# Sixteen columns in place of one for an accumulator output that nobody reads

## The chip, the cores and the metric

The kernel runs on one core of a Trainium2 chip. The metric is the device time of one execution in microseconds, the median over several runs; smaller is better. The core has five engines with queues of their own: TensorE (PE in the profile; its weight loads are shown apart as PEld), VectorE (DVE), ScalarE (ACT), GpSimd (POOL) and SyncE (SP, which only issues transfers here). Each runs its queue in order, and they wait for one another by semaphores.

## The reference, cut to what matters

The input is `x`, 8 batches of 64 x 16 tokens with 128 channels (1024 tokens per batch). Layer 0 is an attention with 8 heads and two softmaxes in a row, a layer norm, a feed-forward part and a layer norm. Layer 1 is an additive attention over all pairs of tokens, and then a recurrent part over the tokens:

```python
def _L1_attn_ref(B, W, v):
    Wi = jnp.einsum('bnd,ed->bne', B, W)
    scores = jnp.einsum('d,bijd->bij', v, jnp.tanh(Wi[:, None, :, :] + Wi[:, :, None, :]))
    attn = jax.nn.softmax(scores, axis=-1)
    return jnp.einsum('bij,bjd->bid', attn, B)
...
x = _L0_conv_ref(x, ...)
t = _to_tokens(x)
t = t + _L1_attn_ref(_ln_t(t), L1_attn_W, L1_attn_v)
t = t + _L1_ffn_ref(_ln_t(t), L1_ffn_W, L1_ffn_V, L1_ffn_gamma, L1_ffn_beta)
```

The scores of layer 1 need a tanh for every pair of tokens and every channel. They are symmetric in the two tokens, so the kernel computes about half of them: 8 batches x some 524,000 pairs x 128 channels.

## The kernel before

Channels lie on the 128 partitions. For one batch, `wiT` holds the projected tokens, 128 x 1024. A row of layer 1 is one token i: its column of `wiT` is added to the columns of all tokens from i on, the tanh of the sum is taken, and TensorE multiplies by `v` (L1175) and collects the scores of 32 tokens per quarter in the PSUM tile `sa`. The function `group` records the rows in groups of 4 k: k rows for each of four row residues c, where k grows from 1 to 8 as the rows get shorter. All rows of a group lie side by side in a stretch of the SBUF ring `th`, which has room for 20 x 1024 columns.

The sum and the tanh of a row can be made in three ways:

- ScalarE does both in one instruction, the tanh with the token's column as bias (`tanh_row`, L1097).
- GpSimd adds k rows at once with one tensor_tensor (`add_rows`, L1107). ScalarE then takes the tanh of whole filled stretches at once (`wide_tanh`, L1155).
- VectorE adds, for k of 4 or more, k rows with the same tensor_tensor (L1107 again), and for smaller k row by row with tensor_scalar (`add_row`, L1101). L1155 then takes the tanh.

The row-wise form has an `accum_out`: besides the sum, the instruction also writes the total of the row to one column per partition. Nobody reads it. On the chip such an operation is shown as two records, `TENSOR_SCALAR_CACHE_REDUCE` for the row and `DVE_READ_ACCUMULATOR` for the total. The column was the last one of an otherwise little used statistics tile:

```python
unused = stats[5][:, 3, 8:9]
...
nc.vector.tensor_scalar(
    rows(c)[:, r, :], wiT[:, i0 + begin[c] :], w_i(c, r), 0.0, ALU.add, ALU.add, accum_out=unused
)
```

The framework that turns the program into instructions puts a semaphore wait wherever an instruction writes what an earlier one wrote or reads, also where both are on the same engine. An instruction that needs more waits than it can carry gets a separate semaphore instruction (`EVENT_SEMAPHORE`) ahead of it.

Who does which part, and in which order, is settled at build time. The class `Plan` collects all operations of both layers with a cost per engine, a priority and their dependencies; `emit` then plays them through and issues each in the order in which it starts in the plan. So layer 0 of the next batch runs between the groups of layer 1 of this batch. Layer 0's VectorE work is the column sums and divisions of the softmaxes (L946, L947, L950, L963, L964), copies out of PSUM (L865), bias adds (L909), and sums into `zs` (L995); its ScalarE work is the exponentials (L942, L960); GpSimd divides again (L974); TensorE makes the scores (L939), the transposes (L853) and the attention products (L988). In layer 1 ScalarE also takes the exponentials of the finished scores (L1271), VectorE takes the reciprocal of the denominator (L1308), and layer norms run over VectorE (L812, L813, L822) and GpSimd (L816, L817, L827). Transfers hardly matter: the queues' share of the 16 transfer engines is 2.3% of the span.

Batch 0's layer 0 runs alone at the start (to about 400 us); the last batch's layer 1 has no layer 0 beside it (from about 4850 us on); the recurrent part of all batches follows from 5300 us.

Of the kernel before, what the change touches and what calls it, by code (L numbers as in the profile page):

```python
# [11 lines left out]
ALU = mybir.AluOpType  # L12
# [3 lines left out]
P = 128  # L16
# [597 lines left out]
@with_exitstack  # L614
def kernel(ctx: ExitStack, tc: tile.TileContext, a: dict):

    fits = ctx.enter_context(tc.tile_pool(name="flag", bufs=1)).tile(
        [1, 1], mybir.dt.int32, tag="fits", name="fits"
    )
    fast_path(tc, a, fits)
    fit = tc.nc.values_load(
        fits[0:1, 0:1], min_val=0, max_val=1, skip_runtime_bounds_check_because="it is a comparison's result"
    )
    with tc.If(fit == 0):
        names = "x wq wk wv wo bq bk bv bo ln1_g ln1_b w1 b1 w2 b2 ln2_g ln2_b wa va wf vf gamma beta out"
        general_path(tc, *[a[n] for n in names.split()])  # L630
# [3 lines left out]
def fast_path(ctx: ExitStack, tc: tile.TileContext, a: dict, fits):  # L634
# [22 lines left out]
    work = main.enter_context(tc.tile_pool(name="work", bufs=1))  # L657
    psum = main.enter_context(tc.tile_pool(name="psum", bufs=1, space=PSUM))

    def tile_of(pool, name, shape):  # L660
        return pool.tile(shape, F32, tag=name, name=name)

    def ring(name, n, shape, pool=work):
        return [tile_of(pool, f"{name}{i}", shape) for i in range(n)]
# [135 lines left out]
    stats = ring("stat", 7, [P, 4, 9])  # L800
# [36 lines left out]
    count = {"aT": 0}  # L837
# [232 lines left out]

                add(("POOL", 2.2), affine2, r=[kg], w=[kg], pri=L0)

    unused = stats[5][:, 3, 8:9]

    def group(it, at0, r0, k, wiT, all_wi, L1, ROWS, fillers, chain, left, both, first_half):

# [4 lines left out]
        i0 = it * P  # L1081
# [3 lines left out]
        begin = [0 if r0 == 0 else 4 * r0 + c for c in range(4)]  # L1085
# [3 lines left out]
        def rows(c):  # L1089
            return slot()[:, at[c] : at[c + 1]].rearrange("p (r n) -> p r n", r=k)  # L1090

        def w_i(c, r=None):
            j = i0 + 4 * r0 + c
            return wiT[:, j : j + 4 * k - 3 : 4] if r is None else wiT[:, j + 4 * r : j + 4 * r + 1]

        def tanh_row(c, r):
            nc.scalar.activation(rows(c)[:, r, :], wiT[:, i0 + begin[c] :], AF.Tanh, bias=w_i(c, r))  # L1097

        def add_row(c, r):

            nc.vector.tensor_scalar(  # L1101
                rows(c)[:, r, :], wiT[:, i0 + begin[c] :], w_i(c, r), 0.0, ALU.add, ALU.add, accum_out=unused
            )

        def add_rows(eng, c):
            shape = [P, k, w - begin[c]]
            eng.tensor_tensor(  # L1107
                rows(c), wiT[:, i0 + begin[c] :].unsqueeze(1).to_broadcast(shape),
                w_i(c).unsqueeze(2).to_broadcast(shape), ALU.add,
            )  # L1110
# [3 lines left out]
        work = {  # L1114
            "ACT": lambda c: (k * (0.18 + 0.833e-3 * (w - begin[c])), lambda: [tanh_row(c, r) for r in rows_of]),
            "POOL": lambda c: (0.27 + 1.62e-3 * k * (w - begin[c]), lambda: add_rows(nc.gpsimd, c)),
            "DVE": lambda c: (k * (0.21 + 1.05e-3 * (w - begin[c])), lambda: [add_row(c, r) for r in rows_of])
            if k < 4
            else (0.15 + 1.04e-3 * k * (w - begin[c]), lambda: add_rows(nc.vector, c)),
        }  # L1120
# [32 lines left out]
        def wide_tanh(_):  # L1153
# [5 lines left out]
            wide_tanh, r=[("rows", g, c) for c in range(4)], w=[("tanh", g)], pri=ROWS - 0.02,  # L1159
# [418 lines left out]
```

## Time and profile before

| What | Value |
|---|---|
| median of 3 runs | 5390.36 us (5388.69 to 5394.67) |
| profiled execution | 5390.73 us |
| its span | 5388.9 us |
| granted TensorE clock, mean | 0.985 |
| busy share PE, DVE, ACT, POOL | 94%, 92%, 95%, 84% |
| instructions on VectorE | 8448 |
| rows at L1101 | 1822, each with an accumulator read |
| separate semaphore instructions at L1101 | 913 |

The profile is of one execution. A group line names the source line, the engine, the operation and its tiles, then how often it occurs, its busy time and mean duration, and the engine's idle time ahead of it with what ended most of that. The chain of waits is followed back from the last instruction: at each step to what released it, or to the instruction ahead of it on its engine. "issue" in it is time in which the engine waited for nothing that the profile shows.

### The profile page before, as it was taken

The numbers are of one execution on the slowest core, as the hardware profiler recorded it, in microseconds if no ns is written. First come the engines' busy times: TensorE is split into PE (matmuls) and PEld (weight loads), VectorE is DVE, ScalarE is ACT, GpSimd is POOL, SyncE is SP. The second block draws the span as 40 slices with busy tenths as digits, with TensorE's granted clock in tenths as the row PEclk, the third lists the DMA queues.
The fourth block names the chain that finished last, engine by engine and source line by source line (L and its number), as shares of the span: only waits on it lengthen the run. The fifth ranks groups of instructions, "written<-read, shape, count | busy, mean of one in ns | idle before, by whom it ended". The sixth has DMA issues, their size and how long they took to land.

```text
span 5388.9 us, 99191 instructions
## 1 busy us (share of the span) xinstructions
PE 5048.0 (94%) x39173; PEld 2782.9 (52%) x39173; DVE 4961.5 (92%) x8448; ACT 5093.6 (95%) x4180; POOL 4536.0 (84%) x3114
## 2 busy tenths in 40 slices
PE   9999999999999999999999999999999999986567
PEld 6655555555555555555555555555555455542125
DVE  7998999999999999999999999999999999988886
ACT  5489999999999999999999999999999999999994
POOL 2364889988998899989999999989999998986992
PEclk9999999999999999999999999999999999998998
DMA  2000000000000000000000000000000000000001
GB/s 62 1 5 1 1 1 5 1 9 1 1 5 5 5 1 1 5 9 1 1 5 5 5 1 1 5 5 5 1 1 5 5 1 1 5 26 7 1 1 68
DMA packets 27339, 37.71 MB, mean 7 GB/s; under 512 B 2512, under 2 KB 19280, under 8 KB 26864
## 3 DMA queue, kind: packets, MB, share of 16 engines
q1 hardware_dynamic: 24832, 27.99, 1.6%
q8 instruction: 310, 5.08, 0.4%
q10 hardware_dynamic: 1872, 3.16, 0.2%
q14 instruction: 165, 1.35, 0.1%
q0 software_dynamic: 160, 0.13, 0.0%
HBM read 19.22 MB, written 12.06 MB: 6 GB/s over the span
## 4 chain that ended last, share of the span: by engine, by line
PE 67%; DVE 15%; ACT 12%; issue 4%; POOL 1%; DMA 0%; DVEq 0%; SPq 0%; ACTq 0%; POOLq 0%
PE sa L1175 24%; PE m L988 13%; PE sc L939 13%; PE m L853 8%; ACT th L1155 6%; DVE th L1101 6%; ACT th L1097 3%; DVE stat_e L963 2%; PE m L917 2%; PE m L1304 2%; DVE stat_e L946 2%; DVE wx L950 1%; PE m L903 1%; DVE aT L865 1%; PE m L1035 1%
## 5 line engine op out<-in xcount | busy, mean ns | idle before, releaser
L1107 POOL TENSOR_TENSOR th<-wiT 128x536 f32<-128x536 f32 (+58 forms) x2304 | 3342.3, 1486 | 244.6 <-PE sa L1175 222.8
L1155 ACT ACTIVATE th<-th 128x2740 f32<-128x2740 f32 (+54 forms) x971 | 2661.2, 2771 | 23.2 <-DVE th L1107 12.3
L1175 PE MATMUL sa<-th,vpat 128*32 128x512 f32 (+32 forms) x24576 | 2030.6, 462 | 212.5 <-ACT th L1155 187.2
L1101 DVE TENSOR_SCALAR_CACHE_REDUCE th<-wiT 128x512 f32<-128x512 f32 (+60 forms) x1822 | 1587.4, 871 | 140.1 <-PE sa L1175 21.9
L1097 ACT ACTIVATE th<-wiT 128x440 f32<-128x440 f32 (+58 forms) x2056 | 1462.7, 782 | 15.1 <-PE sa L1175 14.9
L1175 PEld LDWEIGHTS sa<-th,vpat 128*32 128x32 f32 x24576 | 662.1, 110 | 1341.8 <-issue 850.5
L974 POOL TENSOR_TENSOR wx<-wx,stat_e 128x1024 f32<-128x1024 f32 x512 | 983.2, 1942 | 403.5 <-DVE stat_e L964 360.4
L939 PE MATMUL sc<-xT,wx 128*128 128x512 f32 x2048 | 982.9, 605 | 15.7 <-DVE wx L950 15.3
L988 PE MATMUL m<-aT,wx 128*128 128x256 f32 x3584 | 829.4, 384 | 11.9 <-DVE aT L865 11.9
L988 PEld LDWEIGHTS m<-aT,wx 128*128 128x128 f32 x3584 | 671.1, 191 | 191.9 <-issue 40.7
L946 DVE TENSOR_REDUCE stat_e<-sc 128x16 f32<-128x1024 f32 x512 | 620.4, 1212 | 28.7 <-ACT sc L942 27.8
L950 DVE TENSOR_TENSOR wx<-sc,stat_e 128x1024 f32<-128x1024 f32 x512 | 623.9, 1219 | 23.3
L865 DVE COPY aT<-m 128x512 f32<-128x512 f32 x927 | 600.4, 674 | 34.5 <-PE m L853 32.1
L853 PEld LDWEIGHTS m<-ident,wx 128*128 128x128 f32 x3940 | 445.8, 141 | 326.0 <-issue 162.8
L963 DVE TENSOR_REDUCE stat_e<-wx 128x128 f32<-128x2048 f32 x256 | 583.3, 2278 | 19.0 <-ACT wx L960 18.1
L853 PE MATMUL m<-ident,wx 128*128 128x128 f32 x3940 | 564.4, 278 | 22.5 <-DVE aT L865 12.9
L942 ACT ACTIVATE sc<-sc 128x1024 f32<-128x1024 f32 x512 | 513.7, 1008 | 75.9 <-PE sc L939 71.0
L939 PEld LDWEIGHTS sc<-xT,wx 128*128 128x128 f32 x2048 | 354.9, 190 | 384.3 <-issue 331.4
L960 ACT ACTIVATE wx<-wx 128x2048 f32<-128x2048 f32 x256 | 487.2, 1903 | 21.6 <-DVE wx L950 21.3
L964 DVE RECIPROCAL stat_e<-stat_e 128x128 f32<-128x128 f32 x256 | 244.0, 953 | 8.8
L917 PEld LDWEIGHTS m<-Wvo,xT 128*128 128x128 f32 x1080 | 135.5, 193 | 47.5 <-issue 20.1
L917 PE MATMUL m<-Wvo,xT 128*128 128x128 f32 x1080 | 147.3, 282 | 6.4 <-DVE aT L865 3.0
(183 smaller groups left out, 2899.0 us busy)
## 6 DMA issues: line engine op xcount, KB each, us to landing
xT<-in_xt_dram SPq DMA_DIRECT2D x8, 512.0 KB, 3.5
th<-in_x_dram SPq DMA_DIRECT2D x8, 512.0 KB, 6.9
parked<-X SPq DMA_DIRECT2D x16, 256.0 KB, 2.3
xr<-parked SPq DMA_DIRECT2D x8, 512.0 KB, 7.7
parked_wx<-bT SPq DMA_DIRECT2D x14, 256.0 KB, 2.0
wx<-parked_wx SPq DMA_DIRECT2D x7, 512.0 KB, 3.2
out_dram<-ot ACTq DMA_DIRECT2D x8, 256.0 KB, 2.2
out_dram<-ot SPq DMA_DIRECT2D x8, 256.0 KB, 2.7
```

The lines of the kernel that those rows point to most:

```text
L853: nc.tensor.transpose(bank[:, i * P : (i + 1) * P], s, ident)
L939: nc.tensor.matmul(sc[:, cols], u[:, qt * P : (qt + 1) * P], xT[:, cols], start=True, stop=True)
L946: nc.vector.tensor_reduce(r1, sc.rearrange("p (m g) -> p g m", g=G), AX.X, ALU.add)
L950: nc.vector.tensor_tensor(e3, sc3, r1.unsqueeze(1).to_broadcast([P, M, G]), ALU.mult)
L963: nc.vector.tensor_reduce(r2, e2.rearrange("p q (m g) -> p q m g", g=G), AX.X, ALU.add)
L974: nc.gpsimd.tensor_tensor(e3, e3, r2[:, q, :].unsqueeze(2).to_broadcast([P, M, G]), ALU.mult)
L988: nc.tensor.matmul(bank()[:, :256], vp[:, t, :], aT[:, t, :], start=t == 0, stop=t == NT - 1)
L1097: nc.scalar.activation(rows(c)[:, r, :], wiT[:, i0 + begin[c] :], AF.Tanh, bias=w_i(c, r))
L1101: nc.vector.tensor_scalar(rows(c)[:, r, :], wiT[:, i0 + begin[c] :], w_i(c, r), 0.0, ALU.add, ALU.add, accum_out=unused)
L1107: eng.tensor_tensor(rows(c), wiT[:, i0 + begin[c] :].unsqueeze(1).to_broadcast(shape), w_i(c).unsqueeze(2).to_broadcast(shape), ALU.add,)
L1155: nc.scalar.activation(slot()[:, a:z], slot()[:, a:z], AF.Tanh)
L1175: nc.tensor.matmul(sa[32 * c : 32 * c + 32, s:s1], vpat[:, 31 - r0 - r : 63 - r0 - r], rows(c)[:, r, s - at0 - begin[c] : s1 - at0 - begin ...
```

## The change

The single column is replaced by a tile of 16 columns, `unused`, and each row that VectorE adds takes the next of them in turn. Nothing else is changed; lines below the edit move by 4, so that L1101, L1107, L1155 and L1175 become L1105, L1111, L1159 and L1179. The new tile has 64 bytes per partition and is allocated ahead of the tiles `stat_e`.

```diff
-    unused = stats[5][:, 3, 8:9]
+    unused = tile_of(work, "unused", [P, 16])
+
+    def next_unused():
+        count["unused"] = (count.get("unused", -1) + 1) % 16
+        return unused[:, count["unused"] : count["unused"] + 1]
...
             nc.vector.tensor_scalar(
-                rows(c)[:, r, :], wiT[:, i0 + begin[c] :], w_i(c, r), 0.0, ALU.add, ALU.add, accum_out=unused
+                rows(c)[:, r, :], wiT[:, i0 + begin[c] :], w_i(c, r), 0.0, ALU.add, ALU.add, accum_out=next_unused()
             )
```

## The prediction

> **What bounds the kernel now.** I read the page's engine shares first, then its costliest groups.
>
> ```profile
> PE 5048.0 (94%) x39173; PEld 2782.9 (52%) x39173; DVE 4961.5 (92%) x8448; ACT 5093.6 (95%) x4180; POOL 4536.0 (84%) x3114
> ...
> PE 67%; DVE 15%; ACT 12%; issue 4%; POOL 1%; DMA 0%; DVEq 0%; SPq 0%; ACTq 0%; POOLq 0%
> ...
> L1101 DVE TENSOR_SCALAR_CACHE_REDUCE th<-wiT 128x512 f32<-128x512 f32 (+60 forms) x1822 | 1587.4, 871 | 140.1 <-PE sa L1175 21.9 <-DVE th L1101 16.1 <-issue 2.9
> ```
>
> PE, ACT and VectorE are all nearly full, so the share alone decides nothing. The row touched by the change, L1101, runs 1822 times; VectorE stands idle 140.1 us ahead of it, and the named releasers explain only 41. The busy time by stretch (PE, PEld, DVE, ACT, POOL, then clock, DMA) says more:
>
> ```profile
> 2500.00:3500.00 1000.00, 986.34 (x7928) 542.19 (x7930) 948.49 (x1612) 994.50 (x741) 945.33 (x666) 1.00 0.01 3
> ...
> 5000.00:5100.00 100.00, 59.71 (x544) 16.20 (x536) 89.04 (x158) 100.00 (x34) 93.04 (x59) 0.98 0.00 1
> ```
>
> ACT is the fullest: 994.5 of 1000 us in mid-kernel, all of 5000 to 5200. From 400 to 5300 us ACT is idle for 85 us in all (4900 less the sum of its stretches); before 400 there are few L1101 rows, after 5300 none. The work given to ACT doesn't change, so the change can win what ACT waits, no more. What ends ACT's waits there:
>
> ```profile
> ACT sc L942 <- PE sc L939: 22.9, 30, 2.8
> ACT th L1097 <- PE sa L1175: 14.5, 8, 5.9
> ACT th L1155 <- DVE th L1107: 12.3, 4, 6.8
> ACT E L1271 <- PE sa L1175: 10.5, 9, 2.1
> ACT th L1155 <- DVE th L1101: 7.6, 15, 1.4
> ACT wx L960 <- DVE wx L950: 5.1, 8, 1.5
> ```
>
> VectorE ends 25.0 us of it directly (12.3 + 7.6 + 5.1), PE 47.9 us.
>
> **How rows follow each other.** The timeline of VectorE (start, duration):
>
> ```profile
> 2614.21 1.01 DVE L1101 TENSOR_SCALAR_CACHE_REDUCE th<-wiT 128x768 f32<-128x768 f32 x1 [0.86 <-PE sa L1175]
> 2615.15 0.08 DVE L1101 DVE_READ_ACCUMULATOR th<-wiT 128x1 f32 x1
> 2615.15 0.69 DVE L865 COPY aT<-m 128x512 f32<-128x512 f32 x1
> ...
> 2635.70 0.08 DVE L1101 DVE_READ_ACCUMULATOR th<-wiT 128x1 f32 x1
> 2635.82 1.00 DVE L1101 TENSOR_SCALAR_CACHE_REDUCE th<-wiT 128x749 f32<-128x749 f32 x1
> ...
> 5187.02 0.08 DVE L1101 DVE_READ_ACCUMULATOR th<-wiT 128x1 f32 x1
> 5187.26 0.93 DVE L1101 TENSOR_SCALAR_CACHE_REDUCE th<-wiT 128x689 f32<-128x689 f32 x1
> ```
>
> A copy behind a row starts together with the row's accumulator read, about 0.08 us before the row's recorded end. A row behind a row starts 0.12 us after that start, or 0.24 us where a separate semaphore instruction stands between them. Counted through the trace there are 1180 row-behind-row pairs: 438 without the semaphore instruction (median 0.119 us) and 741 with it (median 0.207), and one odd one. All but that one wait on VectorE's own semaphore.
>
> **What the Trainium skill says.** "Perfetto Trace Analysis", section "DVE / Act Engine Instruction (TENSOR_ADD, Activation, etc)": the next instruction may prefetch once its predecessor has executed, while the semaphore is sent only after the write is acknowledged and then has to propagate. A wait on one's own predecessor therefore costs the tail; the trace agrees, with 0.00 against 0.12 us. "VectorE: DVE Perf Modes", section "The DRAIN you can't avoid", says that a semaphore between VectorE operations costs nothing extra; the trace disagrees by that 0.12 us, and the measurement decides. "SBUF — State Buffer", section "Who interferes with whom": a VectorE operation with two SBUF inputs and a GpSimd operation that reads SBUF lock each other out, while tensor_scalar with its accumulator output stays off the shared port. So rows themselves can't collide with POOL. The L1107 adds on VectorE can; the trace shows one, used below.
>
> **The change, part by part.** The instruction order of all five engines is the same before and after; only waits differ. (1) The 1822 rows and accumulator reads stay, at the same sizes: nothing. (2) Rows that carry a wait on VectorE itself fall from 1418 to 207. Of the 1180 pairs 987 lose it: 403 had no second wait, 322 fall from two or more waits to one and so also lose the semaphore instruction, 262 keep other waits. The remaining 193 waits point to an older row (the column's last use, 16 rows back, or an old ring slot). Behind other instructions an already satisfied wait costs nothing (119 such rows before start at -0.08 us, like those without one), so I take these as free too; if not, 193 x 0.12 to 0.21 = 23 to 40 us of VectorE time stays. (3) 41 other VectorE instructions gain a self-wait that the rows used to cover (20 in L822, 9 in L812, 5 in L1308, seven more): the awaited results are old, so nothing; at the worst 41 x 0.21 = 9 us. (4) The new 16-column tile moves later tiles in SBUF by 64 bytes; no row prices that, I take nothing.
>
> VectorE gains 438 x 0.119 + 741 x 0.207 = 52 + 153 = **205 us** of room. The price of a row behind a row without a wait isn't in the trace: the nearest row is the copy at 0.00. If the accumulator read has to finish first, the start moves by 0.083 us and only 1180 x 0.083 = 98 us less is won; I take the copy's price.
>
> **What of it lies on the path.** The chain of waits, in order of time, shows the pairs like this:
>
> ```profile
> 5180.60 0.03 issue
> 5180.63 0.05 DVEq L1101
> 5180.68 0.06 issue
> 5180.74 0.96 DVE th L1101 x2
> ```
>
> I added up such links over the whole chain: 267, with 26.1 us between rows, and the overlap of 0.083 us each that they also forgo, 22.2: **48 us**, a ceiling. But many lie where ACT is saturated. Taking by stretch the smaller of the chain's links and ACT's idle time: 0.9 (to 400), 0.3 (to 900), 1.7 (to 1500), 4.5 (to 2500), 5.5 (to 3500), 6.6 (to 4500), 4.2 (to 4850), 8.2 (to 5000), 0 (to 5200; the chain has 8.4 here, ACT no gap), 1.8 (to 5300): 34 us, the likely case's upper end.
>
> The forecast goes by ACT's gaps. Of the 25.0 us ended by VectorE, 9.8 (6.82 at 1258.87 and 2.97 at 1451.80) follow L1107 adds slowed down next to POOL, with one row pair or none ahead; they stay. For the other 15.2 I compared each gap with the pairs in VectorE's unbroken run ahead of it: they cover **13**. Of PE's 47.9: in the same span PE's own waits were ended by VectorE for 61 us and by ACT for 215, so 22% or 10.5 us may be VectorE's; not all have pairs ahead, I take three quarters, **8**. Sum 21 us. Against the profiled execution: 5390.7 (span 5388.9 and 1.8 around it) - 21 = **5370 us**; the median of the three runs, 5390.4, is 0.3 lower, which changes nothing. Where these waits go, ACT is late next: its own queue.
>
> **Rivals.** A change of 0.2% is 10.8 us, about what a measurement of this kernel can tell from no change.
>
> *Nothing seen (17%).* The pairs shrink but ACT's gaps stay: PE ends two thirds of them, and the accumulator read may hold the next row after all (0.036 instead of 0.119 us). For it: ACT at 99 to 100% where most pairs are. Against it: the direct gaps at 4828 to 4910, behind dozens of pairs. Gain 0 to 8 us: 5387.
>
> *The whole chain (9%).* ACT's place is taken less strictly than its busy time says and all 48 us come: 5342. Against it: the stretches at 100.00.
>
> *Slower (8%).* VectorE, ahead of its old times, reaches an L1107 add while POOL is in a run, and stands behind the lock:
>
> ```profile
> 1243.81 14.16 POOL L1107 TENSOR_TENSOR th<-wiT 128x862 f32<-128x862 f32 x10
> ...
> 1247.82 10.95 DVE L1107 TENSOR_TENSOR th<-wiT 128x752 f32<-128x752 f32 x1
> ```
>
> This add has 752 elements; one of 756 elsewhere took 0.94 us, so it lost 10.0, and ACT idled 6.8. It ends when POOL's run does. Against the sizes that ran undisturbed (0.15 us + 1.04 ns per element), 21 of the 80 VectorE adds at L1107 lost over 0.5 us, 34 us together. The kernel is slower once the new losses on ACT's path exceed 21 + 11 = 32 us, five such stalls at 6.8: with six, 5370 + 41 = 5411. Against it: the existing stalls can vanish as well as multiply, and POOL is fed by the same slots.
>
> *The change doesn't do what it says*: excluded, the waits of the built program show it.
>
> **How the numbers follow.** The likely case has 66%, with its own range of 8 to 34 us won, 5357 to 5383; 8 of these 66 points win under 10.8 us. Faster by over 0.2%: 58 + 9 = 67%. Within 0.2%: 8 + 17 = 25%. Slower by over 0.2%: 8%. The range goes from 5346, where half the whole-chain case is left out, to 5391, which takes in the case of nothing: some 12 points stay outside.
>
> **What would show it.** Right: separate semaphore instructions at L1101 fall from 913 to about 490; row pairs start 0.00 us after the accumulator read's start; idle time ahead of L1101 falls from 140 us to 30 to 50; L1155 waits for L1101 under 2 us; ACT's idle time between 400 and 5300 falls from 85 to about 64 us while its busy time stays at 5094. Wrong: pairs still 0.1 us apart (the accumulator read holds); ACT's idle time unchanged although VectorE has 200 us more idle time elsewhere (ACT and PE decide); more or longer L1107 adds on VectorE (the lock decides); or ACT's busy time itself changes.

## The result, and the profile after

The changed kernel takes 5374.69 us (median of 14 runs, 5367.16 to 5377.13) against 5389.69 for the kernel before (14 runs beside it): a ratio of 0.9971, interval 0.9963 to 0.9979, 15 us faster. The profiled execution of the changed kernel has a span of 5371.3 us, 17.6 less than before.

From the page, first the engines, then the chain by engine, then two groups of instructions:

```profile
PE 5032.5 (94%) x39173; PEld 2779.7 (52%) x39173; DVE 4889.3 (91%) x8448; ACT 5089.8 (95%) x4180; POOL 4517.5 (84%) x3114
...
PE 68%; ACT 17%; DVE 9%; issue 5%; POOL 1%; DMA 0%; ACTq 0%; SPq 0%; DVEq 0%; POOLq 0%
...
L1105 DVE TENSOR_SCALAR_CACHE_REDUCE th<-wiT 128x512 f32<-128x512 f32 (+60 forms) x1822 | 1500.7, 869 | 78.6 <-PE sa L1179 75.8
```

VectorE's share of the chain falls from 15% to 9%, ScalarE's rises from 12% to 17%. The rows themselves last as long as before (mean 869 against 871 ns). Their group's busy time is lower because it counts overlapping time once: a row now begins while the one ahead still ends. That is the change, seen in VectorE's timeline of the changed kernel:

```profile
5159.15 0.94 DVE L1105 TENSOR_SCALAR_CACHE_REDUCE th<-wiT 128x702 f32<-128x702 f32 x1
5160.02 0.08 DVE L1105 DVE_READ_ACCUMULATOR th<-wiT 128x1 f32 x1
5160.02 0.93 DVE L1105 TENSOR_SCALAR_CACHE_REDUCE th<-wiT 128x700 f32<-128x700 f32 x1
...
5164.32 0.08 DVE L1105 DVE_READ_ACCUMULATOR th<-wiT 128x1 f32 x1
5165.66 0.93 DVE L1105 TENSOR_SCALAR_CACHE_REDUCE th<-wiT 128x692 f32<-128x692 f32 x1 [1.26 <-PE sa L1179]
```

A row starts together with the accumulator read of the row ahead, as the copy did before: 0.00 us in place of 0.12 or 0.24. In the last two lines a row stands 1.26 us, now for TensorE, which has not yet given back the slot in `th`. VectorE's waits for other engines grew: first the kernel before (400 to 5300 us), then the changed one (400 to 5285 us, where layer 1 ends earlier); total, times, longest:

```profile
DVE th L1101 <- PE sa L1175: 21.9, 38, 4.5
DVE aT L865 <- PE m L853: 24.7, 66, 1.7
DVE stat_e L946 <- ACT sc L942: 19.1, 35, 1.6
...
DVE th L1105 <- PE sa L1179: 75.8, 89, 8.0
DVE aT L865 <- PE m L853: 51.4, 113, 1.9
DVE stat_e L946 <- ACT sc L942: 43.0, 69, 2.8
```

These three grew by 104 us together, about half of the 205 us of room: VectorE is ahead and waits. ScalarE has no more to do than before; in the stretches at the end of layer 1 it has almost no gap left (the first line is the kernel before, the others the changed one):

```profile
4850.00:5000.00 150.00, 91.97 (x1070) 34.36 (x1069) 130.29 (x266) 141.79 (x114) 107.77 (x63) 0.83 0.02 6
...
4500.00:4850.00 350.00, 327.25 (x2778) 174.84 (x2774) 322.76 (x705) 349.98 (x278) 316.85 (x237) 0.99 0.04 13
4850.00:5000.00 150.00, 89.77 (x1104) 32.99 (x1096) 127.84 (x273) 147.99 (x109) 102.45 (x68) 0.89 0.01 4
5000.00:5100.00 100.00, 59.71 (x552) 16.52 (x552) 82.22 (x160) 100.00 (x35) 93.94 (x60) 0.98 0.00 1
```

From 4850 to 5000 us ScalarE is busy for 147.99 us (before 141.79). From 400 us to the end of layer 1 it is idle for 73.5 us (before 85.0). What still ends its waits from 400 to 5300 us:

```profile
ACT sc L942 <- PE sc L939: 19.5, 31, 2.8
ACT th L1101 <- PE sa L1179: 14.0, 6, 5.7
ACT th L1159 <- DVE th L1111: 11.9, 3, 6.8
ACT E L1275 <- PE sa L1179: 8.6, 6, 2.7
ACT wx L960 <- DVE wx L950: 2.8, 4, 1.5
...
ACT th L1159 <- DVE th L1105: 1.6, 2, 1.4
```

ScalarE's instructions come in the same order in both kernels, so the same instruction can be compared by its place in the order. Its lead over the kernel before grows in steps: 3.4 us between 1500 and 1700, some 2.1 us each before 2200, 3000 and 3900, 2.4 us from 4500 to 4700, 8.6 us from 4800 to 4900, and 19.0 us in all when the recurrent part begins. Each trace is of one execution, so a part of these steps is chance. How large that part can be is seen in the trace of the kernel with one column (next section), which keeps the waits and takes the time of the kernel before: it leads by 9.5 us at the same place, with steps of 1.8 us between 1500 and 1700, 1.6 before 1900 and 1.7 before 3900, but with none from 4800 to 4900. So the step before 3900 is not the change's. The one from 4800 to 4900 is: with two columns it is 8.2 us.

Between 4400 and 4500 the changed kernel loses 6.2 us. The cause of that loss is seen in GpSimd's and VectorE's timelines (the first two lines) and ScalarE's (the third):

```profile
4392.75 9.62 POOL L1111 TENSOR_TENSOR th<-wiT 128x504 f32<-128x504 f32 x7
...
4394.95 7.94 DVE L1111 TENSOR_TENSOR th<-wiT 128x488 f32<-128x488 f32 x1
...
4402.98 1.87 ACT L1159 ACTIVATE th<-th 128x2000 f32<-128x2000 f32 x1 [2.08 <-DVE th L1111]
```

An add of 488 elements takes 7.94 us because VectorE reached it while GpSimd was in a run of seven. Before, the same add took 1.43 us:

```profile
4407.12 1.43 DVE L1107 TENSOR_TENSOR th<-wiT 128x488 f32<-128x488 f32 x1
```

It is the stall that the rival "slower" named, once, while several short ones vanished (over 0.5 us lost: 21 adds before, 18 after, 34 and 35 us in all). It belongs to the kernels without the waits: this add takes 7.96 us with two columns too, and 1.43 us with one column.

### The profile page after: what moved, and what is told of

Read it like the earlier page. It is cut to its first block, busy times and chain, and to the rows that moved or that the text cites. A ratio compares the mean times of both kernels' runs of the same rounds, so it can differ in the third digit from the quotient of the medians.

```text
span 5371.3 us, 98784 instructions
## 1 busy us (share of the span) xinstructions
PE 5032.5 (94%) x39173; PEld 2779.7 (52%) x39173; DVE 4889.3 (91%) x8448; ACT 5089.8 (95%) x4180; POOL 4517.5 (84%) x3114
## 4 chain that ended last, share of the span: by engine, by line
PE 68%; ACT 17%; DVE 9%; issue 5%; POOL 1%; DMA 0%; ACTq 0%; SPq 0%; DVEq 0%; POOLq 0%
PE sa L1179 25%; PE m L988 13%; PE sc L939 12%; ACT th L1159 10%; PE m L853 7%; ACT th L1101 4%; DVE th L1105 2%; PE m L917 2%; DVE stat_e L963 2%; PE m L1308 2%; ACT sc L942 1%; PE m L903 1%; ACT wx L960 1%; DVE stat_e L946 1%; DVE wx L950 1%
## 5 line engine op out<-in xcount | busy, mean ns | idle before, releaser
L1111 POOL TENSOR_TENSOR th<-wiT 128x536 f32<-128x536 f32 (+58 forms) x2304 | 3338.9, 1483 | 257.3 <-PE sa L1179 218.5
L1159 ACT ACTIVATE th<-th 128x2740 f32<-128x2740 f32 (+54 forms) x971 | 2658.1, 2769 | 15.8 <-DVE th L1111 11.9
L1179 PE MATMUL sa<-th,vpat 128*32 128x512 f32 (+32 forms) x24576 | 2025.3, 461 | 222.4 <-ACT th L1159 198.4
L1105 DVE TENSOR_SCALAR_CACHE_REDUCE th<-wiT 128x512 f32<-128x512 f32 (+60 forms) x1822 | 1500.7, 869 | 78.6 <-PE sa L1179 75.8
L1101 ACT ACTIVATE th<-wiT 128x440 f32<-128x440 f32 (+58 forms) x2056 | 1461.7, 780 | 14.7 <-PE sa L1179 14.5
L1179 PEld LDWEIGHTS sa<-th,vpat 128*32 128x32 f32 x24576 | 662.9, 110 | 1347.6 <-issue 843.4
L988 PE MATMUL m<-aT,wx 128*128 128x256 f32 x3584 | 827.5, 384 | 11.9 <-DVE aT L865 11.9
L950 DVE TENSOR_TENSOR wx<-sc,stat_e 128x1024 f32<-128x1024 f32 x512 | 623.9, 1219 | 23.3
L960 ACT ACTIVATE wx<-wx 128x2048 f32<-128x2048 f32 x256 | 486.7, 1901 | 19.1 <-DVE wx L950 19.1
L1105 DVE DVE_READ_ACCUMULATOR th<-wiT 128x1 f32 x1822 | 151.4, 83 | 0.0
```

Source lines behind the costliest of these rows:

```text
L950: nc.vector.tensor_tensor(e3, sc3, r1.unsqueeze(1).to_broadcast([P, M, G]), ALU.mult)
L988: nc.tensor.matmul(bank()[:, :256], vp[:, t, :], aT[:, t, :], start=t == 0, stop=t == NT - 1)
L1105: nc.vector.tensor_scalar(rows(c)[:, r, :], wiT[:, i0 + begin[c] :], w_i(c, r), 0.0, ALU.add, ALU.add, accum_out=next_unused())
L1111: eng.tensor_tensor(rows(c), wiT[:, i0 + begin[c] :].unsqueeze(1).to_broadcast(shape), w_i(c).unsqueeze(2).to_broadcast(shape), ALU.add,)
L1159: nc.scalar.activation(slot()[:, a:z], slot()[:, a:z], AF.Tanh)
L1179: nc.tensor.matmul(sa[32 * c : 32 * c + 32, s:s1], vpat[:, 31 - r0 - r : 63 - r0 - r], rows(c)[:, r, s - at0 - begin[c] : s1 - at0 - begin ...
```

## The experiments

All ratios are against the kernel before, run beside it on the same chip. "Gain of the change" is the 0.29% above.

| Kernel | Median us | Ratio | Interval |
|---|---|---|---|
| one column in the new tile | 5387.08 | 0.9999 | 0.9991 to 1.0007 |
| two columns | 5369.86 | 0.9967 | 0.9955 to 0.9979 |
| 16 columns, memsets between | 5373.97 | 0.9978 | 0.9967 to 0.9988 |
| 16 columns, rows split | 5382.10 | 0.9990 | 0.9981 to 0.9998 |
| 16 columns, no multi-row adds on VectorE | 5361.59 | 0.9956 | 0.9942 to 0.9969 |
| the same with one column | 5447.26 | 1.0109 | 1.0093 to 1.0124 |
| 16 columns, such adds in the last batch only | 5349.65 | 0.9929 | 0.9915 to 0.9942 |
| 16 columns, planned row price 0.14 | 5338.22 | 0.9902 | 0.9887 to 0.9917 |
| one column, planned row price 0.14 | 5400.24 | 1.0022 | 1.0015 to 1.0028 |
| one column, planned row price 0.30 | 5372.83 | 0.9965 | 0.9952 to 0.9979 |
| 16 columns, 0.14, adds in the last batch only | 5324.59 | 0.9878 | 0.9863 to 0.9893 |
| the same, and the plan knows | 5331.60 | 0.9892 | 0.9876 to 0.9907 |

### Is it the wait on the row ahead?

The new tile with one column:

```diff
-        count["unused"] = (count.get("unused", -1) + 1) % 16
+        count["unused"] = (count.get("unused", -1) + 1) % 1
```

> The new tile of 16 columns is kept, but every row writes its first column. Theory (the wait of a row on the row ahead of it is the cost): 1418 self-waits at L1105 as before, pairs of rows 0.12 and 0.21 us apart, time as before, 5390 within 0.1%. Rival (the place of the output or of the tiles behind it in SBUF matters): the time of the changed kernel, 5375.

Measured: 5387.08, ratio 0.9999; the pairs are 0.118 us apart (438 of them) and 0.206 us (741), as here:

```profile
5160.02 0.08 DVE L1105 DVE_READ_ACCUMULATOR th<-wiT 128x1 f32 x1
5160.25 0.96 DVE L1105 TENSOR_SCALAR_CACHE_REDUCE th<-wiT 128x718 f32<-128x718 f32 x1
```

The shifted tiles behind it in SBUF do nothing that this measurement can see (0.9991 to 1.0007).

Two columns (`% 2`):

> The rows alternate over 2 columns, so that a row waits on the row before the last; 1095 of 1418 self-waits stay. Theory (only a wait on the immediate predecessor costs, because its write is still on the way): pairs 0.00 us apart, all of the gain, 5375. Rival (a self-wait costs by being there, or by its semaphore instruction): with 323 of the 1211 removed waits gone, about a quarter of the gain, 5386.

Measured: 5369.86, ratio 0.9967, all of the gain.

```profile
5160.32 0.08 DVE L1105 DVE_READ_ACCUMULATOR th<-wiT 128x1 f32 x1
5160.32 0.94 DVE L1105 TENSOR_SCALAR_CACHE_REDUCE th<-wiT 128x699 f32<-128x699 f32 x1
```

Most rows still wait on VectorE, now on the row before the last. In some 300 pairs this is the row's only wait, and they start at 0.00 us like the others. Of the 913 semaphore instructions at the rows 808 stay, so these by themselves aren't the cost either. A wait of VectorE on itself was free here once the awaited write was one row old; only the wait on the immediate predecessor cost. Sixteen columns aren't needed for it.

### Is it VectorE's time?

```diff
+    spare = tile_of(work, "spare", [P, 4, 16])
...
+            nc.vector.memset(spare[:, count["unused"] % 4, :], 0.0)
```

> The changed kernel with a memset of 16 columns of a spare tile behind each of VectorE's 1822 rows, the plan unchanged. Estimate from the small memsets of the profile (0.065 us and up, the neighbours overlapping): 0.07 to 0.1 us each, 130 to 180 us of VectorE time put back in place of the 205 us that the waits took. Theory (the gain is VectorE's time at a few places, whatever fills it): most of the gain is lost, 5383 to 5390. Rival (the waits cost in another way than by VectorE's time, or VectorE's time doesn't count): 5375 as with the change.

Measured: 5373.97, and the dose was wrong. In VectorE's timeline of this kernel:

```profile
5183.86 0.08 DVE L1107 DVE_READ_ACCUMULATOR th<-wiT 128x1 f32 x1
5183.88 0.89 DVE L1107 TENSOR_SCALAR_CACHE_REDUCE th<-wiT 128x662 f32<-128x662 f32 x1
5183.90 0.07 DVE L1110 MEMSET spare<- 128x16 f32 x1
```

The memset has a record of 0.07 us, but the next row comes only 0.02 us later than without it. VectorE's busy time is 4907.9 us, 19 more than with the change: a tenth of what the waits took. The run decides nothing.

The second dose splits five of six rows in two:

```diff
-            nc.vector.tensor_scalar(
-                rows(c)[:, r, :], wiT[:, i0 + begin[c] :], w_i(c, r), 0.0, ALU.add, ALU.add, accum_out=next_unused()
-            )
+            count["split"] = count.get("split", -1) + 1
+            n = w - begin[c]
+            h = n // 2 if count["split"] % 6 else n
+            for x0, x1 in ((0, h), (h, n)):
+                if x0 < x1:
+                    nc.vector.tensor_scalar(
+                        rows(c)[:, r, x0:x1], wiT[:, i0 + begin[c] + x0 : i0 + begin[c] + x1], w_i(c, r), 0.0, ALU.add, ALU.add,
+                        accum_out=next_unused(),
+                    )
```

> The changed kernel with five of six of VectorE's rows issued as two halves, each with its own accumulator column: 1518 more instruction pairs at the row's fixed price of 0.135 us (a row of 288 elements lasts 0.437 us from start to start, 1.05 ns per element), 205 us of VectorE time, as much as the waits took, without a wait; the plan is unchanged. The memsets of the run before turned out at 0.02 us each and were too small a dose. Theory (the gain is VectorE's time at a few places): nearly all of the gain is lost, 5383 to 5391. Rival (the waits cost in another way): 5370 to 5376.

Measured: 5382.10, ratio 0.9990. VectorE's busy time is 5071.7 us, 182 more than with the change. Of the gain of 0.29%, 0.10% is left (0.02 to 0.19), so about two thirds are gone, and not less than a third; by the medians alone (5382.10 against 5389.44) it is half. In the step by step comparison, ScalarE's gain from 4800 to 4900 shrinks from 8.6 to 2.4 us. Time on VectorE, without any wait, thus costs a good part of what the waits cost. Why not all is not shown; it would fit the places, since splits fall on all rows, also on those that stand behind another operation, where before there was no wait to take away.

### The lock between VectorE's adds and GpSimd

Rows in place of VectorE's 80 multi-row adds, at the plan's places:

```diff
-            else (0.15 + 1.04e-3 * k * (w - begin[c]), lambda: add_rows(nc.vector, c)),
+            else (0.15 + 1.04e-3 * k * (w - begin[c]), lambda: [add_row(c, r) for r in rows_of]),
```

> The changed kernel, but VectorE's 80 multi-row adds (L1111) are issued as single rows with the accumulator output, at the places and costs of the same plan. By the price of a row (0.135 us + 1.05 ns per element) that is 416 more rows and about 44 us more than the adds cost undisturbed, against 34 us that they lose next to GpSimd. Theory (the lock's stalls lie on ScalarE's path, 11.9 us of its idle time, and are what differs from execution to execution): 5363 to 5370, and the spread of the runs shrinks. Rival (these stalls are made up for later, and the extra rows are not): 5375 to 5380.

Measured: 5361.59, ratio 0.9956, a little better than expected; the spread of the five runs did not shrink (5358.70 to 5367.24), so the lock is not what differs from execution to execution. From 900 to 1500 us ScalarE no longer waits for an add (9.8 us with the change). At the end it waits more (ScalarE's waits, 4850 to 5000 us; with the change this line is missing):

```profile
ACT th L1159 <- DVE th L1105: 10.0, 5, 3.0
```

The same with one column (`% 1` besides):

> Rows in place of VectorE's 80 multi-row adds, as in the run without the lock, but with all rows on one column, so that each waits on the row ahead. Theory (the two effects are separate: the adds' lock gives 8 us, the waits 16 us, and the 416 further rows now pay 0.12 to 0.21 us, 50 to 87 us of VectorE time, most of it after 4850 us): 5380 to 5388. Rival (all of the gain of the run without the lock comes from the adds): 5362 to 5370.

Measured: 5447.26, 1.1% slower than before; the theory missed it by 59 us, the rival by 77. I had priced the waits of the 416 further rows as if VectorE had room for them; half of the rows (208) stand in the last batch, where it has none. The stretch from 4850 to 5000 us of this kernel, and what ScalarE waits for in it:

```profile
4850.00:5000.00 150.00, 74.64 (x837) 31.76 (x837) 130.62 (x587) 92.95 (x100) 46.70 (x42) 0.65 0.03 8
...
ACT th L1159 <- DVE th L1105: 57.0, 17, 8.7
```

Short rows, several to a group, directly behind one another: ScalarE is busy for 93 of 150 us and waits 57 for VectorE's rows. The columns are worth 86 us here (5447 less 5362), 15 in the kernel as it was.

That is only half of the miss. ScalarE's order is the same as in the run at 5362, so the delay can again be laid beside the waits of the row pairs, place by place (times of the run at 5362). Up to 4800 us, 167 us of waits delay ScalarE by 43 us, about a quarter; from 4800 to 4925 us, 43 us of waits delay it by 44; from there to the recurrent part, 59 us of waits by nothing. So VectorE's waits count one for one where ScalarE stands for VectorE's rows, not at all where ScalarE has no gap, and in part between.

Rows in the first seven batches, adds in the last:

```diff
-            else (0.15 + 1.04e-3 * k * (w - begin[c]), lambda: add_rows(nc.vector, c)),
+            else (0.15 + 1.04e-3 * k * (w - begin[c]), lambda: [add_row(c, r) for r in rows_of] if L1 < 6.5 else add_rows(nc.vector, c)),
```

> The changed kernel with rows in place of VectorE's multi-row adds in the first seven batches only (40 of the 80 adds); the last batch, whose rows have no layer 0 beside them, keeps its adds. In the run without the lock ScalarE's idle time from 4850 to 5000 us rose from 2 to 16 us. Theory (the adds' lock costs in the middle, the further rows cost at the end): 5348 to 5356. Rival (the idle time at the end is made up for in the recurrent part or by the place of the stretch): 5360 as in the run without the lock.

Measured: 5349.65, ratio 0.9929, as the theory said: adds behind the lock cost in the middle, further rows cost at the end.

```profile
4850.00:5000.00 150.00, 86.20 (x979) 28.14 (x979) 126.33 (x240) 147.67 (x100) 112.10 (x69) 0.91 0.00 1
```

ScalarE is back at 147.67 us in this stretch (134.76 with rows everywhere).

### What the plan believes a row costs

The plan gives work to VectorE at a price of 0.21 us + 1.05 ns per element for a row. Without the wait a row takes 0.135 us + 1.05 ns per element, with it 0.25 to 0.34 us. Lowered to 0.14, with 16 columns:

```diff
-            "DVE": lambda c: (k * (0.21 + 1.05e-3 * (w - begin[c])), lambda: [add_row(c, r) for r in rows_of])
+            "DVE": lambda c: (k * (0.14 + 1.05e-3 * (w - begin[c])), lambda: [add_row(c, r) for r in rows_of])
```

> The changed kernel, with VectorE's price for a row in the plan lowered from 0.21 + 1.05 ns per element to 0.14, what the pairs now take. The plan gives VectorE 105 more rows (1927) and the order changes everywhere. Theory (ScalarE is the limit, so taking some 100 fixed starts of 0.18 us off it gives up to 19 us): 5355 to 5370. Rival (a new order shifts waits at random and hides this): 5365 to 5395.

Measured: 5338.22, ratio 0.9902, 17 us faster than the range of the theory. The page shows where a part of the gain comes from:

```profile
PE 5024.6 (94%) x39173; PEld 2779.7 (52%) x39173; DVE 4946.0 (93%) x8667; ACT 5074.0 (95%) x4096; POOL 4449.0 (83%) x3057
```

ScalarE has 84 instructions fewer (4096 in place of 4180; its own rows at L1101 fall from 2056 to 1968), which saves it 15.8 us; the rest of the 33 us between the two profiled spans (5371.3 and 5338.6) is less idle time of ScalarE. VectorE is fuller than with the change, as the lower price asks.

The same plan with one column:

```diff
-        count["unused"] = (count.get("unused", -1) + 1) % 16
+        count["unused"] = (count.get("unused", -1) + 1) % 1
```

> The plan with VectorE's row price at 0.14, as in the run at 5338, but with all rows on one column, so that each waits on the row ahead. Theory (the lower price pays only where the rows really take it; each pair now takes 0.12 to 0.21 us more than planned, and the plan has filled VectorE up): 5365 to 5400. Rival (the gain at the lower price is a luckier order and has nothing to do with the waits): 5338 plus the change's own 15 us, 5353 or less.

Measured: 5400.24, ratio 1.0022, at the edge of the theory's range and far from the rival's. ScalarE's waits for VectorE's rows are 27.5 us here and 2.8 us in the run at 5338. Under one and the same plan the columns are worth 62 us.

One column (`% 1`) with a price close to what its rows take:

```diff
-            "DVE": lambda c: (k * (0.21 + 1.05e-3 * (w - begin[c])), lambda: [add_row(c, r) for r in rows_of])
+            "DVE": lambda c: (k * (0.30 + 1.05e-3 * (w - begin[c])), lambda: [add_row(c, r) for r in rows_of])
```

> One column, and VectorE's row price in the plan raised to 0.30, close to what a row behind a row takes with its wait (0.135 + 0.12 to 0.21); 1704 rows. Theory (a plan with the true price loses less to waits; ScalarE gets some 100 rows more at 0.18 us): within 15 us of the kernel before, 5375 to 5395, its idle time from 4850 to 5000 us smaller. Rival (any change of the order moves the time by tens of us): outside of that.

Measured: 5372.83, ratio 0.9965. That is 2 us below the theory's range and so on the side of the rival, and what the theory said of the waits did not come: ScalarE's idle time from 4850 to 5000 us is 9.9 us (before 8.2), and VectorE's rows, adds and divisions (L950) end 26.0 us of its waits (before 25.0). So a plan with another price gained as much as the change did under the old one, but that it did so by pricing the waits is not shown; it may be the order.

What the prices show together is that the low one pays only without the waits: with one column 0.14, 0.21 and 0.30 took 5400, 5387 and 5373 us, with 16 columns 0.14 and 0.21 took 5338 and 5375. Each price was one order.

The two gains together. First the edits of the run at 5349.65 and of the run at 5338.22 in one kernel:

> The 16 columns, the row price of 0.14, and rows in place of VectorE's multi-row adds in the first seven batches, without the plan knowing of the latter. Theory (the two gains are separate; the lock cost 20 us with the plan of the change): 5318 to 5333. Rival (with the new plan the lock's stalls lie elsewhere or off the path): 5335 to 5345.

Then with a plan that knows of the rows:

```diff
-            if k < 4
+            if k < 4 or L1 < 6.5
...
-                w=[("rows", g, c)], pri=ROWS, take=None if c else slot, port=k >= 4,
+                w=[("rows", g, c)], pri=ROWS, take=None if c else slot, port=k >= 4 and L1 > 6.5,
```

> As the run with row price 0.14 and rows in the first seven batches, but the plan knows that these are rows: it prices them as rows and no longer keeps GpSimd and VectorE apart for them; 2325 rows. Theory (a plan that knows the prices is at least as good): 5315 to 5333. Rival (orders scatter by more than that): up to 5350.

Measured: 5324.59 (0.9878) and 5331.60 (0.9892), four runs each, both in the ranges of their theories; their intervals overlap, so that the plan gains by knowing of the rows is not shown. The first has the lowest median, 65 us under the kernel before.

## Why the prediction was right

It said 5370 us and faster; the runs said 5374.7, a gain of 15 us where 21 were forecast.

- **The price of the waits was right.** The pairs start at 0.00 us, the copy's price; the accumulator read doesn't hold the next row. The semaphore instructions at the rows fall from 913 to 490. The 193 pairs that kept a wait, and the 41 other instructions that gained one, cost nothing that shows: the median distance is 0.00 for each kind of pair, and the 41 start behind the instruction ahead as before (median 0.08 us before its end in both kernels). Of the 1180 pairs, 81 are over 0.1 us apart, 76 of them because they wait for TensorE.
- **ScalarE's gaps were the right measure.** 205 us of room on VectorE became 15 us of time, because ScalarE, not VectorE, sets the end. The chain's 48 us were a ceiling that was not reached: from 5000 to 5200 us the chain ran through VectorE's rows, but ScalarE was busy for 200 of 200 us, and the 35 us of row waits that the kernel with one column has there, and the changed one has not, cost ScalarE 0.0 us. The forecast sign, idle time of ScalarE from 85 to about 64 us, came in part: it is 73.5.
- **The direct gaps: 13 us forecast.** The waits of L1155 for rows fell from 7.6 to 1.6 us, of L960 for L950 from 5.1 to 2.8; 8.3 us by the profile's count of waits (5.8 against the trace with one column, which has 5.3 and 4.9). Those behind L1107 went from 12.3 to 11.9. This was said to stay, and its sum did, but the parts changed: short gaps after 4850 us went, and the stall at 4395 came.
- **The gaps ended by PE: 8 us forecast.** They went from 47.9 to 42.1 us, so 5.8. But the trace with one column, which keeps the waits, has 43.1 on the same three lines, so all but 1.0 us of this may be chance: this term is not shown. (Its share of 22% left out the small lines of the view; with them VectorE ended 67 us of PE's waits and ScalarE 218, 24%.)
- **What was mis-sized** are these two terms and one that had no place in the sum: the new stall behind the lock, 6.2 us on ScalarE's path. Without it this pair of executions would stand at some 24 us, an estimate (17.6 + 6.2). That the total came as near as 15 to 21 is in part luck, then: one of its two terms isn't shown, and an unforeseen loss stands against the gains. The rival that ended slower had its mechanism right and its number wrong: one new stall came, not six.
- **One size was wrong:** the idle time ahead of the rows was to fall from 140 to 30 to 50 us; it is 78.6, nearly all of it (75.8) waits for slots in `th`, which L1179 gives back.

The main cause, the wait on the immediate predecessor, is shown by the runs with one and two columns; that VectorE's time at a few places is what counts, by the split rows and by the end stretch of the run at 5447. Three things stay open. A third to a half of the gain is not lost to the split rows, and only their places were argued for it. Why a plan with the higher price gains with one column is not known.

And runs of the same kernel gather at levels some 5 us apart (5367, 5371 and 5376 for the changed one); removing the adds' lock did not remove this. The levels go with the granted clock: the seven runs from 5376.3 to 5377.1 us had 0.988, the seven faster ones 0.989 or 0.990. No run shows which of the two follows from the other. Between the two profiles the clock rose from 0.985 to 0.989, but the clock alone doesn't make the gain: runs of the kernel before at 0.988, beside the later kernels, took 5382.1 to 5386.3 us. And from 4850 to 5000 us, where it rose most (0.83 to 0.89), TensorE ended only 1.3 us of ScalarE's waits in either trace.

## What to carry to other kernels

An output that nobody reads is still written, and two instructions that write it to the same place wait for one another: give it two places in turn. What such a saving is worth is read from the gaps of the engine that sets the end, in each stretch, and not from the time saved on the engine that is relieved. Where a plan or a fixed split decides who does the work, correct the plan's price along with the wait: 15 us without, 51 us with it here.

## What the runs showed of the hardware that was not expected

- A wait of a row on the row before the last cost 0.00 us, on the last row 0.12 us, and 0.21 us with a semaphore instruction between.
- A memset of 128x16 between two rows, 0.07 us by its record, moved the next row by 0.02 us.
- An add on VectorE can stand until the end of a whole run of GpSimd instructions that follow without a gap: it lost 7.3 us behind most of a run of seven, and 10.0 us behind one of ten. It isn't always so: in the changed kernel an add of 760 elements at 1429.42 us took 2.18 us and ended 0.8 us after the GpSimd instruction that it met, although another one followed that without a gap. What decides between the two is not shown.
